# A transformer layer's hand-made instruction order: other due times for a round trip through DRAM, vector pieces between tensor pieces, another order at a seam

## The chip, the cores and the metric

The kernel runs on one core of a Trainium2 chip, with one launch. The metric is the device time of that core in microseconds (us); a profile of one execution shows what each engine did. The engines are TensorE (PE; its weight loads are shown apart as PEld), VectorE (DVE), ScalarE (ACT), GpSimd (POOL) and SyncE (SP, which here only issues DMAs). Each engine works through its own list of instructions in the order in which the program wrote them.

## The reference

Four sequences of 1024 tokens with 256 channels go through causal attention with 16 heads of 16 channels and a linear position bias, then through an encoder layer whose attention runs across the four sequences at one position, and whose feed-forward part sends each token to one of eight experts.

```python
x = L0_attn_x                                        # (4, 1024, 256)
x = x + _L0_attn_ref(_layernorm(x), w_attn, w_proj)  # causal, alibi bias, 16 heads
x = x + _L0_ffn_ref(_layernorm(x), ...)

# in _L0_ffn_ref, with T, B, C = x.shape
attn = softmax(einsum('tbhd,sbhd->bhts', q, k) * scale)
h = _layernorm(x + (ctx @ out_w.T + out_b), ln1_g, ln1_b)
_, top_i = jax.lax.top_k(softmax(flat @ router_w.T + router_b), 2)
assign = jnp.max(top_i, axis=-1)
for e in range(E):
    he = gelu(flat @ w1[e].T + b1[e]); oe = he @ w2[e].T + b2[e]
    out = where((assign == e)[:, None], oe, out)
return _layernorm(h + out, ln2_g, ln2_b)
```

(`T` is 4 there and `B` is 1024, since the encoder takes the first axis as time: its attention has four steps.)

## The kernel before

**Attention.** The queries are cut into 20 units. Units 0 to 11 are 256 queries of one sequence, units 12 to 15 the first 128 of the last 256, units 16 to 19 the other 128; four units, one for each sequence, make a position range. A unit goes through four groups of four heads. `score` multiplies keys by queries (tile `sk`) and ACT takes the exponential (`p`); `weigh` multiplies `p` by the values (`pv`) and ACT copies the result to `yt`. Along with the weighted values comes one row for each head that holds the sum of its exponentials.

**The sums' way through DRAM.** A unit's result is divided by those sums and projected. The sums lie in a few rows of `yt` and are wanted in every row, so they go through DRAM: `yt` is stored to `y`; `load_sums` loads the sums; `invert` takes the reciprocal on DVE (`inverse`) and stores it to `r`; `load_y` loads `r`, spread over the rows (`su`), and the values (`yc`); `divide` multiplies the two on DVE; `project` multiplies by the output weights on PE (`op`) and adds to `x` on DVE. All these loads and stores stand in SP's list. The last unit, 19, takes another way: `normalise(g)` spreads each group's sums with a product on PE (`sum`), takes a reciprocal and multiplies on DVE (`yn`), and `project_slots` projects. Its groups 0 and 1 do so in the loop, groups 2 and 3 after it. `load_sums(19)` is issued all the same, for a test of the sums' size at the end.

**Encoder.** Once all four units of a position range are projected, its blocks of 128 positions by four sequences can start as fronts. There are eight, 0 to 7; the last, front 7, waits for unit 19. A front is a generator that yields pieces with a kind and a cost: kind E and P for DVE, R for a root on POOL, N and A for ACT, D and d for PE. In order they are: statistics, root, normalised `u`, its transposition `ut`, q, k and v in four pieces (`qkvp`, copied to `qkv` by ACT and DVE), four scores (`pr`, `sc`), a softmax, four weightings (`pv<-qkv,sc`, `ctx`), the transposition `ct`, output projection (`ao`), a second normalisation, the routing (`key`, `before`, `equal`, `rank`, `hot`), its place among its expert's tokens (`place`). There is one `qkv` buffer: a front that wants to start its q, k, v (kind DQ) waits until the front that holds it has done its weightings. At most two fronts are under way at a time. The first six fronts admit the first table of expert tiles (`tabulate_first`, product `who_first`), and front 7 the second (`tabulate_rest`, product `who`).

**What sets the order.** The program writes the instructions in an order that an ordering model chooses while the program is built. The model has clocks for PE, DVE and ACT (`time`), advanced by the costs of the pieces. The loop goes through places: two scores, one weighing, and around them `E_slot` and `D_slot`. `attended(u, at)` puts a unit's five steps down with due times `at + SUMS_BY` and so on; `E_slot` does the DVE and DMA steps that have come due on the model's PE clock, and `D_slot` the projections that have, then calls `take_D`, which takes PE pieces of the fronts until a place holds 10 us of them (`D_SLOT`). `take_E` takes the fronts' DVE, ACT and POOL pieces that are ready, as long as the model's DVE clock is at most 1 us ahead of PE's. In the loop, `take_E` is called at the end of each `E_slot` and once after `D_slot`.

**After the loop** comes what is still due, then the rest of unit 19, and then front 7, what is left of the other fronts and of the first table, and the tiles of the experts, ordered by a second loop. A tile gathers its rows with an indirect DMA of POOL (`given`), runs `mtp`, `hid` and `oe` on PE, a normalisation on DVE with its root on POOL, and is scattered with another indirect DMA (`out_dram`).

Of the kernel before, what the change touches and what calls it, by code (L numbers as in the profile page):

```python
# [41 lines left out]
G = H // 4  # L42
# [30 lines left out]
D_SLOT = 10.0  # L73
SWITCH, COLUMN, EXP_AT_ALL, EXP, READ = 0.2, 1 / 600, 0.17, 1 / 1200, 0.7
AHEAD, EARLY_BY, ROOT, OF_D = 1.0, 0.2, 1.4, 0.35
SUMS_BY, INVERTED_BY, Y_BY, DIVIDED_BY, PROJECTED_BY = 7.0, 14.0, 18.0, 29.0, 31.0

EXP_ZERO = -126 * math.log(2.0)

# [526 lines left out]
def fast_layer(ctx: ExitStack, tc: tile.TileContext, odd, x, wq, wk, wv, wp, w_in, w_out, w_r,  # L606
# [60 lines left out]
    def bank(name):  # L667
        if tail_banks:
            return tail_banks[0].tile([P, QC], F32, tag="m", name=name)
        if half_of:  # L670
            return half_of.pop()
        pair = pair_of_banks(name)
        halves[pair.tensor.name] = [], []
        half_of.append(pair[:, 1])
        return pair[:, 0]
# [388 lines left out]
    def load_sums(u):  # L1064
        part_of_row = units[u][2] * H
        issue_stores(("y", u))
        nc.sync.dma_start(
            sums[u], heads_of(u)[:, D].rearrange("h (k w) -> h k w", w=part_of_row)
        )
# [65 lines left out]
    def normalise(g):  # L1135
        if g % 2 == 0:
            held["yn", g // 2] = ends.tile([P, 2, W], F32, tag="su", name=f"yn_{g}", bufs=2)
        yt, yn = (held[k, g // 2][:, g % 2, :P] for k in ("yt", "yn"))
        pm = bank(f"sum_{g}")[:, :P]
        nc.tensor.matmul(pm, slot_sum, yt, start=True, stop=True)  # L1140
        nc.vector.reciprocal(yn, pm)
        nc.vector.tensor_tensor(yn, yn, yt, ALU.mult)
# [894 lines left out]
    queue, running = [], []  # L2037
# [12 lines left out]
    def busy(on, cost, ready=0.0):  # L2050
        time[on] = max(time[on], ready) + cost
        return time[on]

    def on_tensor(cost):
        return busy("PE", cost, max([0.0] + [pair_free[k] for k in taken]))

    def read_at(when):
        for k in taken:
            pair_free[k] = when
        taken.clear()  # L2060

    def product(cost, what):
        taken.clear()
        what()
        end = on_tensor(cost)
        busy("DVE", OF_D * cost, end - 0.5 * cost)
        read_at(max(end + READ, time["DVE"]))
        return end

    def start_fronts():  # L2070
        if queue and len(running) < 2:
            issue_stores(*[it[0] for it in stores if it[0][0] == "u"])
        while queue and len(running) < 2:
            running.append(Running(queue.pop(0)))

    def take_E(some=True):

        start_fronts()
        left = some
        while left:  # L2080
            left = False
            for it in list(running):
                now, kind = time["PE"], it.kind
                if kind not in ("E", "N", "R", "P"):
                    continue
                on = {"E": "DVE", "P": "DVE", "N": "ACT"}.get(kind)
                if it.ready > max(now, time[on] if on else 0.0) + EARLY_BY:
                    continue
                if on == "DVE" and time["DVE"] > now + AHEAD:
                    continue  # L2090
                if kind == "R":
                    it.ready = max(now, it.ready) + ROOT
                else:
                    it.ready = busy(on, it.cost if on == "DVE" else 0.5, it.ready)
                left = True
                it.next()
                if it.kind == "end":
                    running.remove(it)

    def take_D(cost):  # L2100

        for it in list(running):
            while it.kind[0] in "Dd":
                if it.kind == "DQ" and ("qkv",) in held:
                    break
                if it.kind != "d" and it.ready > time["PE"] + EARLY_BY:
                    break
                if cost and cost + it.cost > D_SLOT:
                    break
                if it.kind == "DQ":  # L2110
                    held["qkv",] = True
                cost += it.cost
                end = product(it.cost, it.next)
                it.ready = max(end + READ, time["DVE"])
            if it.kind == "end":
                running.remove(it)

    begins = [0]
# [32 lines left out]
    due_E, due_D = [], []  # L2151
# [19 lines left out]
    def pop_due(due, now):  # L2171
        some = sorted((it for it in due if it[0] <= now), key=lambda it: it[0])
        for it in some:
            due.remove(it)
        return [(cost, what) for _, cost, what in some]
# [43 lines left out]
    def E_slot(k, some=True):  # L2219
        for cost, what in of_E.pop(k, []) + pop_due(due_E, time["PE"]):  # L2220
            what()
            busy("DVE", cost)
        issue_stores(age=1)
        for it in stores:
            it[1] += 1
        load_next()
        if tables and fetching:
            experts.fetch()
        take_E(some)

    def D_slot(p):
        todo = of_D.pop(p, []) + pop_due(due_D, time["PE"])
        for cost, what in todo:
            product(cost, what)
        take_D(sum(cost for cost, _ in todo))

    for p in range(-6, 0):
        E_slot(2 * p)
        D_slot(p)
        E_slot(2 * p + 1)  # L2240
# [9 lines left out]
    def score_next(k):  # L2250
        u, g, r = rounds[k]
        taken.clear()
        waiting.append((u, g, r, score(u, g, r)))
        end, n = on_tensor(SWITCH + columns_of(u, r) * COLUMN), columns_of(u, r)
        for pair in list(taken):
            pair_free[pair] = busy("ACT", EXP_AT_ALL + 2 * n * EXP, end)
        if r == n_rounds(u) - 1 and u < last_unit:
            to_fill.append((u + 1, g))

    def weigh_next(some):  # L2260
        taken.clear()
        weigh(some)
        end = on_tensor(SWITCH + sum(columns_of(u, r) for u, _, r, _ in some) * COLUMN)
        read_at(busy("ACT", 0.4, end))
        u, g, r, _ = some[-1]
        if g == G - 1 and r == n_rounds(u) - 1:
            attended(u, time["ACT"])

    def fill():
        while to_fill:  # L2270
            fill_slots(*to_fill.pop(0))

    for p in range(len(rounds) // 2):
        then = p < len(rounds) // 2 - 1
        score_next(2 * p)
        E_slot(2 * p)
        D_slot(p)
        fill()
        take_E(then)
        score_next(2 * p + 1)  # L2280
        if len(waiting) > 2:
            weigh_next(waiting[:2])
            del waiting[:2]
        fill()
        E_slot(2 * p + 1, then)
# [5 lines left out]


    assert not of_E and not of_D, (sorted(of_E), sorted(of_D))
    for _, what in pop_due(due_E + [], 1e9) + pop_due(due_D + [], 1e9):
        what()
    for it in running:
        it.ready = 0.0
    for g in range(2, G):
        normalise(g)
    load_sums(last_unit)  # L2300
    project_slots()
    tail = ctx.enter_context(pool("tail", 1))
# [55 lines left out]
    def begin(it):  # L2358
        if it.kind == "DQ" and ("qkv",) in held or it.kind[1:] == "C" and part.placed < NT - 1:
            return 1e9  # L2360
        return max(it.ready, free[engine_of[it.kind[0]]])
# [27 lines left out]
    while threads:  # L2389
# [4 lines left out]
        at, _, it = min((begin(it) + FIRST_BY * n, n, it) for n, it in enumerate(threads))  # L2394
# [26 lines left out]
@with_exitstack  # L2421
def tile_layer(ctx: ExitStack, tc: tile.TileContext, *args):
    nc = tc.nc
    flag = ctx.enter_context(tc.tile_pool(name="flag", bufs=1))
    odd = flag.tile([P, 1], I32, tag="odd", name="odd")
    fast_layer(tc, odd, *args)
    again = nc.values_load(
        odd[0:1, 0:1], min_val=0, max_val=1,
        skip_runtime_bounds_check_because="a comparison's result",
    )  # L2430
    with tc.If(again > 0):
        general_layer(tc, *args)
# [75 lines left out]
```

## Time and profile before

| | us |
|---|---|
| runs | 824.45, 828.9, 827.63 |
| median | 827.63 |
| the profiled execution | 827.67 |
| its span, first to last instruction | 825.9 |
| busy in the span: PE, PEld | 708.6, 532.4 |
| busy in the span: DVE, ACT, POOL | 544.8, 416.5, 253.6 |
| last `pv` product starts | 617.66 |
| unit 19 added to `x` | 632.57 |
| `who_first` | 642.87 |
| `who` | 731.59 |

A row of the profile's groups or its order of time gives start and duration, the engine, the line of the code, the operation, and what it writes and reads; in brackets stands how long the engine was idle before it and what ended the idle time. Most lines are given as L587, since a helper issues nearly all instructions; the tiles' names tell them apart. A busy PE isn't PE at its peak, and the share of busy time over the whole span mixes stages that have different limits.

### The profile page before, as it was taken

Reading aid. Unit: us, or ns where it says so; the run is one execution under the profiler, and the core shown is the slowest. Engines: PE = TensorE matmul, PEld = TensorE weight load, DVE = VectorE, ACT = ScalarE, POOL = GpSimd, SP = SyncE. Lnnn points to the kernel's source line nnn. Section 1 sums busy time; section 2 is a strip of 40 time slices with the busy share of each in tenths; the row PEclk is TensorE's granted clock in tenths of the full one; section 3 lists DMA queues with packets and bytes.
Section 4 is the critical chain, followed back from the end, with each engine's and each line's share of the span. In section 5 each row is a group of like instructions: output and inputs, shape, how many; then the busy total and the mean of one; then the engine's idle time right before and its main releaser. Section 6 shows DMA issues by size and latency. Waiting matters only on the chain. (4 is left out here: it accounts for less than half of the span.)

```text
span 825.9 us, 22497 instructions
## 1 busy us (share of the span) xinstructions
PE 708.6 (86%) x8917; PEld 532.4 (64%) x8917; DVE 544.8 (66%) x1316; ACT 416.5 (50%) x625; POOL 253.6 (31%) x360
## 2 busy tenths in 40 slices
PE   3988878999999999998998998999983689677882
PEld 2766656667666656565787876788662368566771
DVE  7335403739489768847966648497684779885663
ACT  1554535647547656635665757487550236233540
POOL 5533211313021222111222211122120235638885
PEclk9899898999999999999999999999995699988996
DMA  7444444435234234423554556255125512234430
GB/s 218 120 149 147 115 126 139 137 98 169 82 105 136 91 97 127 131 74 98 140 157 118 163 162 158 57 156 166 36 75 198 178 47 89 89 96 127 128 97 25
DMA packets 75220, 99.57 MB, mean 121 GB/s; under 512 B 19496, under 2 KB 58723, under 8 KB 74596
## 3 DMA queue, kind: packets, MB, share of 16 engines
q1 hardware_dynamic: 62272, 67.84, 28.3%
q10 hardware_dynamic: 7972, 16.05, 6.2%
q0 software_dynamic: 4864, 14.16, 5.7%
q8 instruction: 73, 1.20, 0.7%
q14 instruction: 39, 0.32, 0.1%
HBM read 61.55 MB, written 35.12 MB: 117 GB/s over the span
## 5 line engine op out<-in xcount | busy, mean ns | idle before, releaser
L587 ACT ACTIVATE p<-sk 128x1024 f32<-128x1024 f32 (+1 forms) x320 | 287.8, 939 | 160.6 <-PE sk L587 139.4
L1005 POOL TENSOR_SCALAR_AFFINE_SELECT p<-p 128x512 f32<-128x512 f32 (+1 forms) x160 | 105.6, 664 | 396.6 <-ACT p L587 394.6
L587 PE MATMUL sk<-slots 32*128 32x128 f32 (+1 forms) x3456 | 181.1, 328 | 21.5 <-DVE kq L587 8.4
L587 PEld LDWEIGHTS sk<-slots 32*128 32x128 f32 x3456 | 137.2, 187 | 65.0 <-issue 24.8
L587 PE MATMUL pv<-p,v 128*32 128x128 f32 (+1 forms) x3456 | 143.4, 312 | 9.9 <-DVE count L587 2.9
L587 PEld LDWEIGHTS pv<-p,v 128*32 128x32 f32 x3456 | 95.9, 110 | 46.9 <-issue 7.8
L587 PE MATMUL qkvp<-w_in,ut 128*128 128x264 f32 (+1 forms) x228 | 80.3, 488 | 0.0
L587 PEld LDWEIGHTS qkvp<-w_in,ut 128*128 128x128 f32 x228 | 40.8, 193 | 26.9 <-issue 22.4
L587 PE MATMUL oe<-w,ge 128*128 (+1 forms) x152 | 43.4, 410 | 14.4 <-DVE given L587 6.0
L587 PE MATMUL qkp<-xt,wqk 128*128 128x256 f32 x224 | 55.5, 392 | 0.2 <-ACT p L587 0.2
L1839 POOL DMA_INDIRECT given<-rows,rows x38 | 43.5, 1144 | 27.4 <-DVE at_t L587 11.4
L587 DVE COPY qkv<-qkvp 128x264 f32<-128x264 f32 x28 | 12.1, 432 | 54.1 <-PE qkvp L587 54.1
L587 PEld LDWEIGHTS qkp<-xt,wqk 128*128 128x128 f32 x224 | 40.9, 191 | 10.5 <-issue 3.3
L587 PE MATMUL hid<-mt,w 128*128 128x128 f32 x304 | 47.2, 293 | 0.4 <-ACT ge L587 0.4
L587 ACT COPY qkv<-qkvp 128x512 f32<-128x512 f32 (+1 forms) x29 | 16.1, 557 | 59.0 <-PE qkvp L587 47.1
L587 PEld LDWEIGHTS hid<-mt,w 128*128 128x128 f32 x304 | 42.2, 201 | 1.9 <-ACT ge L587 0.9
L1955 POOL DMA_INDIRECT out_dram<-o,out_rows x38 | 38.9, 1024 | 8.7 <-issue 5.9
L587 DVE TENSOR_TENSOR pv<-qkv,sc 128x1024 f32<-128x1024 f32 x32 | 40.2, 1257 | 0.6 <-PE ctp L587 0.6
L587 DVE TENSOR_REDUCE sc<-pr 128x64 f32<-128x1024 f32 x32 | 39.0, 1220 | 1.1
L587 DVE TENSOR_TENSOR pr<-qkv 128x1024 f32<-128x1024 f32 x32 | 39.6, 1238 | 0.0
L587 PEld LDWEIGHTS oe<-w,ge 128*128 128x128 f32 x152 | 27.2, 200 | 19.1 <-DVE given L587 7.4
L587 PE MATMUL vp<-wv,xt 128*128 128x256 f32 x128 | 34.4, 414 | 0.0
(316 smaller groups left out, 1017.9 us busy)
## 6 DMA issues: line engine op xcount, KB each, us to landing
slots<-k SPq DMA_DIRECT2D x128, 80.0 KB
k<-kq SPq DMA_DIRECT2D x32, 256.0 KB
v<-v ACTq DMA_DIRECT2D x4, 1152.0 KB
x<-in_x_dram SPq DMA_DIRECT2D x16, 256.0 KB
y<-yt SPq DMA_DIRECT2D x16, 256.0 KB
rows<-x SPq DMA_DIRECT2D x32, 128.0 KB
slots<-k SPq DMA_DIRECT2D x64, 64.0 KB
rows<-u SPq DMA_DIRECT2D x8, 512.0 KB
```

The costliest lines, as they stand in the source:

```text
L587: ins = made(*args, **kwargs)
L1005: nc.gpsimd.affine_select(blocks, blocks, pattern=[[0, 2], [0, size], [1, P]], compare_op=ALU.is_ge, fill=0.0, base=0, channel_multiplier=-1,)
L1839: nc.gpsimd.indirect_dma_start(out=self.hx, out_offset=None, in_=t.rows_of, in_offset=bass.IndirectOffsetOnAxis(ap=t.rows_[:, self.j:self. ...
L1955: ins = nc.gpsimd.indirect_dma_start(out=out.rearrange("t n c -> (t n) c"), out_offset=bass.IndirectOffsetOnAxis(ap=t.table.out_rows[:, t. ...
```

## The change

It has three parts. The five due times of a unit's way become shorter. `take_D` calls `take_E` after each PE piece that it takes, where before only the end of the place did; `some` says whether vector pieces may be taken (not in the last place of the loop). And after the loop, `normalise(2)` and `normalise(3)` are written ahead of the projections that are still due, but behind the loads and divisions that are still due; before, they stood behind both.

```diff
-SUMS_BY, INVERTED_BY, Y_BY, DIVIDED_BY, PROJECTED_BY = 7.0, 14.0, 18.0, 29.0, 31.0
+SUMS_BY, INVERTED_BY, Y_BY, DIVIDED_BY, PROJECTED_BY = 5.0, 10.0, 12.5, 19.0, 20.5

-    def take_D(cost):
+    def take_D(cost, some):
         for it in list(running):
             while it.kind[0] in "Dd":
...
                 cost += it.cost
                 end = product(it.cost, it.next)
+
                 it.ready = max(end + READ, time["DVE"])
-            if it.kind == "end":
+                take_E(some)
+            if it.kind == "end" and it in running:
                 running.remove(it)

-    def D_slot(p):
+    def D_slot(p, some=True):
         todo = of_D.pop(p, []) + pop_due(due_D, time["PE"])
         for cost, what in todo:
             product(cost, what)
-        take_D(sum(cost for cost, _ in todo))
+        take_D(sum(cost for cost, _ in todo), some)

         E_slot(2 * p)
-        D_slot(p)
+        D_slot(p, then)
         fill()

-    for _, what in pop_due(due_E + [], 1e9) + pop_due(due_D + [], 1e9):
+    for _, what in pop_due(due_E + [], 1e9):
+        what()
+    for g in range(2, G):
+        normalise(g)
+    for _, what in pop_due(due_D + [], 1e9):
         what()
     for it in running:
         it.ready = 0.0
-    for g in range(2, G):
-        normalise(g)
     load_sums(last_unit)
     project_slots()
```

## The prediction

> **What bounds the kernel now.** I read first the page's slices and a table of windows, which share the run out by stage, then the waits of VectorE (DVE) inside attention, then the order of time around the seam between attention and the last stage. The kernel has three regimes: attention to about 620 us, a seam of 12 us, and a last stage of some 200 us. The columns of the table are: stretch, its length, then busy us of PE, PEld, DVE, ACT, POOL with instruction counts, the granted clock, the DMA share and GB/s.
>
> ```profile
> 500.00:620.00 120.00, 111.76 (x2384) 89.65 (x2384) 88.42 (x187) 75.70 (x99) 24.80 (x39) 0.99 0.37 105
> 620.00:632.00 12.00, 6.20 (x24) 4.75 (x16) 3.19 (x6) 0.27 (x1) 0.00 (x0) 0.50 0.62 214
> 632.00:666.00 34.00, 19.31 (x80) 10.82 (x79) 24.82 (x66) 6.49 (x12) 5.49 (x5) 0.74 0.45 153
> 666.00:732.00 66.00, 54.61 (x364) 47.17 (x364) 59.11 (x159) 29.42 (x63) 32.34 (x33) 0.92 0.28 84
> 732.00:800.00 68.00, 53.59 (x381) 46.58 (x378) 43.88 (x138) 27.59 (x61) 54.73 (x75) 0.95 0.39 118
> ```
>
> Attention belongs to PE (111.8 of 120 us), and DVE has 31.6 us to spare there. From 632 to 732 us it is DVE: 83.9 of 100 us, and in its second part 59.1 of 66. From 732 us it is POOL (54.7 of 68), which gathers rows for the expert tiles and scatters results. The chain that ended last says the same: it can be followed back only to DVE's work at 716 us, goes through the `who` product of the second table at 731.6 us, and from there along POOL. So the end is set by when `who` can run, and `who` needs the routing of the last encoder block, front 7.
>
> Next, DVE's waits between 200 and 620 us (who waited, for whom: us in all, times, longest):
>
> ```profile
> DVE qkv L587 <- PE qkvp L587: 45.4, 21, 6.1
> DVE yc L587 <- DMA yc<-y: 12.5, 4, 5.8
> DVE inverse L587 <- DMA sums<-y: 4.9, 2, 3.8
> ```
>
> DVE's idle time in attention is mostly that inside a run of encoder products: PE projects q, k, v token group by token group and DVE has nothing queued between the copies. Meanwhile encoder vector work is queued behind that run, and what is left of it at 620 us is done in the DVE-bound stage. The order of time shows both ends:
>
> ```profile
> 587.01 0.43 DVE L587 COPY qkv<-qkvp 128x264 f32<-128x264 f32 x1 [0.37 <-PE qkvp L587]
> 589.73 0.43 DVE L587 COPY qkv<-qkvp 128x264 f32<-128x264 f32 x1 [2.29 <-PE qkvp L587]
> 592.45 0.43 DVE L587 COPY qkv<-qkvp 128x264 f32<-128x264 f32 x1 [2.29 <-PE qkvp L587]
> 592.80 0.18 DVE L587 TENSOR_REDUCE best<-key 128x4 f32<-128x32 f32 x1
> ...
> 617.66 2.74 PE L587 MATMUL pv<-p,v 128*32 128x128 f32 x64 [2.86 <-DVE count L587]
> 620.45 0.27 ACT L587 COPY yt<-pv 128x128 f32<-128x128 f32 x1 [5.24 <-PE pv L587]
> ...
> 625.67 0.43 DVE L587 TENSOR_TENSOR yc<-yc,su 128x256 f32<-128x256 f32 x1 [6.71 <-DMA yc<-y]
> 628.71 0.96 DVE L587 RECIPROCAL yn<-sum 128x128 f32<-128x128 f32 x1
> 632.57 0.42 DVE L587 TENSOR_TENSOR x<-x,op 128x256 f32<-128x256 f32 x1 [1.38 <-PE op L587]
> ...
> 642.44 1.22 DVE L587 TENSOR_TENSOR pv<-qkv,sc 128x1024 f32<-128x1024 f32 x1
> 655.51 1.07 ACT L587 COPY qkv<-qkvp 128x512 f32<-128x512 f32 x2 [11.81 <-DVE pv L587]
> ```
>
> Two gaps of 2.29 us stand between copies, then a burst of vector work. After 620 us DVE waits 6.7 us for unit 18's `yc`. Front 6's weighting (`pv<-qkv,sc`, four times from 642.44) comes after the end of attention, and ACT waits 11.8 us to copy front 7's q, k, v, because the one `qkv` buffer is still read by front 6.
>
> **What the Trainium skill says.** "PSUM — Partial Sum Buffer", Engine vs sequencer instructions: the queues of ScalarE, VectorE and GpSimdE are strict FIFO. The trace agrees: vector work ready before 587 us stands behind the copies and starts at 592.80. "DMA: Bandwidth & Descriptors", Anatomy of one DMA: a semaphore wait happens on the issuing sequencer before dispatch, and a DMA on GpSimd's path has about 2.0 us fixed. Here, on SP's queue, unit 18's `r` store was issued at 618.99 and the first load that needs it at 621.19 us: 2.2 us. "Perfetto Trace Analysis", Optimization Strategy: with several regimes, interleaving them may help; the table above shows the regimes.
>
> **The change part by part.** (1) The due times set only the order of instructions. From a unit's last weighing, sums, inverse, loads, division and projection now come at 5, 10, 12.5, 19, 20.5 instead of 7, 14, 18, 29, 31 of the model's us. A place of the schedule costs the model 4 us (single-block units: two scores of 0.2+512/600 and a weighing of 0.2+1024/600) to some 13 us (with encoder products), so 10.5 us are one or two places. Fronts 4, 5 and 6, which start from the projections of units 11 and 15, can start that much earlier. What the way itself needs, from the trace: store issue 0.4, landing 2.2, issue 0.55, landing 2.2, reciprocal 0.24 to 0.35, issue 0.35, landing 2.2, four loads 2.5, landing 2 (yc issued by 623.7, divided at 625.67), about 13 us. The order fits on average. Where two steps fall into one visit, DVE waits; the bounds are nothing and 3.8 us for an inverse, 5.8 us for a division (the longest waits above).
>
> (2) Vector pieces are now taken between products. No instruction is added. A gap of 2.29 us is about one score or weighting piece (1.22+1.22 us, or 1.22+0.69+0.42). Over 200 to 620 us 45.4 us of gaps can be filled. The cost: a PSUM copy queues behind up to one such piece, 2.4 us, while PE has other bank pairs to write; without that cover PE waits 2 us for each of the 28 qkv copies on DVE, 56 us at the very worst; I take nothing.
>
> What follows from (1) and (2): each front holds the one `qkv` buffer for less time, and 4, 5 and 6 follow one another through it. By the model's own order of the kernel before, front 6 takes `qkv` about four places before the end of attention, and fronts 4 and 5 hold it seven places each. One to two places from the start of front 4, and about one saved per hold, put front 6 three to four places further on: through its softmax and weighting, up to its `ct`. Front 5, whose end admits the first table, ends about three places earlier, so that table falls into attention too.
>
> Moved out of the last stage, from DVE's rows of 633 to 658 us: top and subtract 1.0, softmax sums 1.5, four weightings of 1.22+0.69+0.42 = 9.3, copy of `ct` 0.7, first table 1.3+2.0+1.5+2.6 = 7.4: 19.9 us. DVE is 84% busy there, so I pass on three quarters, 15 us. The 11.8 us wait for `qkv` is part of this, not added to it. Against it, front 7 finishing earlier leaves about one more tile for POOL after `who`: an out 1.0, a gather 1.1, a memset 0.1, half a root 0.4, gaps 0.3: 2.9 us. Last stage: -12 us (bounds -20, -3).
>
> PE work moved into attention: eight transposes of `ct`, 1.9 us, and `who_first`, 1.3 us. Against this stand the 2.9 us that PE waited for DVE at 617.66, if that backlog goes. Attention: +2 us (bounds -4, +8).
>
> (3) The seam. Today 620.72 (end of the last `yt` copy) to the `x` addition at 632.57 is 11.9 us: wait for `yc`, project unit 18 (2.05), then the sums of groups 2 and 3, two reciprocals with products (628.71 to 631.19), last products. Now the sums come first, 1.1 us of PE, and the 2.5 us of DVE run beside unit 18's projection; with `yc` there the `x` addition follows at 620.7+1.1+2.5+1.4 = 625.7, 6.9 us sooner. If `yc` is as late as today, PE still stands before unit 18's products until 626.2, and only 1 us is won. The loads are due at 12.5 rather than 18, so they go out a visit or two before the end: I take -5 us (bounds -7, -1). SP's loads of expert weights behind `load_sums` aren't needed before 668 us.
>
> Sum: +2 - 12 - 5 = -15 us against the profiled execution's 827.67 us (span 825.9 plus 1.8 around), which stands at the median of 827.63: 812.7, so 813 us. Its own range is 803 to 823.
>
> **The rivals.** *Given back after `who`*: earlier routing finds more tiles of the first table undone; five more at 2.9 us eat 14.5 of the 15 us, which leaves +2 - 5 = -3: about 825 us. For it: POOL is 80% busy after 732 us. Against: the first table comes earlier too, and POOL stands idle for most of 620 to 670 us.
> *The order hardly moves*: front 6 stands where it stood, since `qkv` and not the projection holds it. 827 us. For it: front 5 waits for the buffer for several places. Against: part (2) shortens just those holds.
> *Slower, DVE waits for landings in attention*: if inverse and division fall into one visit with their loads for most of the 19 units, DVE loses 3.8+5.8 = 9.6 us a unit, 182 us instead of the 50 us of today (30.7 for sums, 19.2 for `yc`). The PSUM copies stand behind it; at one fifth reaching PE, 132 us more make +26 us. Then the forecast's -15 is overrun: 827.67+26-15, about 839 us. It decides once these waits pass about 125 us in all (75 more at a fifth make 15). For it: steps of 5 and 6.5 us are shorter than a place with encoder products. Against: in 200 to 620 us PE waited only about 11 us for DVE (its own table of waits), so most such stalls were absorbed. That the code doesn't do what it says I leave at almost nothing.
>
> **How the numbers follow.** Forecast 0.50, given back 0.16, order unmoved 0.14, slower 0.20. The range 801 to 833 takes in the first three and the near end of the fourth. What a measurement here can tell from no change is 0.5%, 4.1 us: below 823.5 lie nearly all of the forecast and a part of the second, 0.62; between 823.5 and 831.8 the rest of these and the third, 0.18; above, the fourth, 0.20.
>
> **What would show it.** Right: waits `qkv<-qkvp` of DVE clearly under 45 us; `who` about 15 us or more before 731.6; front 6's weighting and `who_first` before the last `pv`; no 11.8 us wait of ACT; sums before unit 18's `op`. Wrong: `sums` and `yc` waits of DVE over 125 us, PE's busy share of 200 to 620 us falling under 93%, the last `pv` later than 628 us, or as long a way as today from the last `pv` to `who`.

## The result, and the profile after

The changed kernel takes 855.52 us (median of 4 runs, 850.01 to 863.67) against 827.15 us for the kernel before beside it: a ratio of 1.0324, with a 95% interval of 1.0257 to 1.039. One of the four runs, 863.67 us, was in a slower state of the chip; the ratios here, and the medians from here on, leave such runs out. The change costs some 27 us, where a gain of 14 us, 813 us, was foretold.

The table of windows by stage, first of the kernel before and then of the changed one. Columns: stretch, length, busy us of PE, PEld, DVE, ACT and POOL with instruction counts, granted clock, DMA share, GB/s. The cuts are the end of the last `yt` copy (the end of attention) and the start of the product `who`.

```profile
0.00:620.70 620.70, 565.06 (x8019) 414.32 (x8019) 402.19 (x914) 350.06 (x482) 146.59 (x223) 0.98 0.43 125
620.70:731.50 110.80, 79.22 (x440) 62.27 (x440) 86.62 (x230) 35.44 (x76) 37.83 (x38) 0.82 0.37 120
731.50:826.00 94.50, 64.29 (x459) 55.83 (x458) 56.03 (x173) 31.01 (x69) 69.13 (x99) 0.90 0.30 94
```

```profile
0.00:663.90 663.90, 581.07 (x8043) 426.94 (x8043) 412.39 (x948) 349.75 (x483) 147.33 (x224) 0.95 0.40 117
663.90:761.40 97.50, 75.43 (x417) 60.57 (x418) 75.56 (x196) 35.20 (x75) 35.49 (x38) 0.89 0.41 136
761.40:855.70 94.30, 64.82 (x458) 55.85 (x458) 56.57 (x173) 30.56 (x69) 69.22 (x99) 0.90 0.31 94
```

Attention is 43.2 us longer (663.9 against 620.7), the stretch from there to `who` 13.3 us shorter (97.5 against 110.8), and what follows `who` the same. 43.2 - 13.3 - 0.1 = 29.8, which is the difference of the two spans (855.7 - 825.9). The profiled execution took 857.52 us, some 4 us more than the median of those kept. So the loss is all in attention, and a gain is where one was expected. Inside attention PE's idle time rose from 620.7 - 565.1 = 55.6 to 663.9 - 581.1 = 82.8 us, 27.2 more; the other 16.0 us are busy time, for only 24 matmuls more (the first table, 0.81 us together). The granted clock tells why: its mean fell from 0.98 to 0.95. In the trace's records of that clock it is at half for 68.3 us of attention against 25.9 before, and PE is busy in those stretches for 51.4 us against 18.8; a projection product takes 634 ns there and 379 otherwise (last section), so an estimate of the loss is 40 to 50% of the difference, 13 to 16 us. The split into idle and busy is exact only to some 7 us: seam_only, below, has the same order in attention as the kernel before, and shows 571.9 us busy at 0.96 (before 565.1 at 0.98), with attention ending at 620.1.

Next the waits, from 20 us to the end of attention, of DVE and then of PE (who waited, for whom: us, times, longest). First the kernel before:

```profile
DVE qkv L587 <- PE qkvp L587: 54.1, 25, 6.1
DVE inverse L587 <- DMA sums<-y: 30.7, 6, 14.6
...
DVE yc L587 <- DMA yc<-y: 12.5, 4, 5.8
```

```profile
PE xtp L587 <- DVE xn L587: 4.2, 3, 3.2
PE qkp L587 <- DVE xn L587: 3.6, 1, 3.6
```

Then the changed one:

```profile
DVE yc L587 <- DMA yc<-y: 57.2, 10, 9.9
DVE qkv L587 <- PE qkvp L587: 41.8, 21, 2.3
...
DVE inverse L587 <- DMA sums<-y: 20.9, 6, 5.7
...
DVE yc L587 <- DMA sums<-y: 7.7, 1, 7.7
```

```profile
PE xtp L587 <- DVE xn L587: 16.7, 5, 8.8
PE qkp L587 <- DVE yc L587: 8.5, 3, 5.7
PE vp L587 <- DVE yc L587: 6.3, 1, 6.3
...
PE router L587 <- DVE yc L587: 2.4, 1, 2.4
PE op L587 <- DVE yc L587: 2.2, 1, 2.2
```

A wait for several signals is put down to the one that came last, so a wait of the division (`yc`) can stand under another load's name, as `sums` here. DVE's waits for landings (`yc` and `inverse`) went from 43.2 to 85.8 us. PE waited 7.8 us for `xn` and 1.7 for `yc` before; now 16.7 and 19.4. (`qkp`, `vp`, `router` and `xtp` name the PSUM bank: the product that reads `yc` is the projection, whichever bank it gets.) Its waits for other work of DVE fell from 23.7 to 13.8 us, so that DVE held up PE for 49.9 us in all, 33.2 before.

One place shows the whole thing. The order of time of the changed kernel, cut to one unit's way and to what waited ("..." stands for lines left out):

```profile
298.60 0.34 DVE L587 RECIPROCAL inverse<-sums 128x32 f32<-128x32 f32 x1
...
298.97 0.34 SPq L1075 DMA_DIRECT2D r<-inverse  x1
300.44 0.60 SPq L1090 DMA_DIRECT2D su<-r  x1
...
302.35 0.57 SPq L1093 DMA_DIRECT2D yc<-y  x1
...
306.79 0.69 DVE L587 TENSOR_TENSOR yc<-yc,su 128x512 f32<-128x512 f32 x1 [7.85 <-DMA yc<-y]
307.40 1.38 DVE L587 TENSOR_SCALAR u<-u,mv_h,rstd_h 128x256 f32<-128x256 f32 x4
...
309.80 0.73 DVE L587 TENSOR_SCALAR xn<-x,mv_x,rstd_x 128x256 f32<-128x256 f32 x2
...
310.36 1.13 PE L587 MATMUL xtp<-ident,xn 128*128 128x128 f32 x4 [8.82 <-DVE xn L587]
```

The reciprocal, its store, the four loads and the division stand back to back in the program. The last load was issued at 302.35 us and DVE's next instruction after the reciprocal is the division, which starts at 306.79: 7.85 us in which DVE does nothing. Behind it stand four `u`, five small instructions and then `xn`, the normalised rows that PE is to transpose next. PE's next product needs `xn`, and PE stands 8.82 us. The windows around it, with the columns of above:

```profile
295.00:301.50 6.50, 6.45 (x111) 4.12 (x100) 3.70 (x15) 5.40 (x7) 2.99 (x4) 1.00 0.17 43
301.50:310.00 8.50, 0.04 (x2) 0.00 (x0) 3.10 (x11) 1.51 (x2) 1.28 (x2) 0.63 0.30 96
310.00:315.00 5.00, 4.64 (x24) 3.71 (x28) 4.27 (x15) 0.58 (x1) 0.00 (x0) 0.61 0.37 108
315.00:320.00 5.00, 5.00 (x67) 3.23 (x60) 3.91 (x7) 3.70 (x5) 0.00 (x0) 1.00 0.29 103
```

PE is busy 0.04 of 8.5 us, and then works at a mean clock of 0.61 for five more: part of the stall is paid a second time in slow products.

The seam, in order of time:

```profile
663.65 0.27 ACT L587 COPY yt<-pv 128x128 f32<-128x128 f32 x1 [1.91 <-PE pv L587]
663.80 0.57 SPq L1093 DMA_DIRECT2D yc<-y  x1
...
668.00 0.43 DVE L587 TENSOR_TENSOR yc<-yc,su 128x256 f32<-128x256 f32 x1 [5.47 <-DMA yc<-y]
...
673.07 0.42 DVE L587 TENSOR_TENSOR x<-x,op 128x256 f32<-128x256 f32 x1 [1.72 <-PE op L587]
```

Unit 18's last load goes out at 663.80, after the last copy of attention, and DVE waits 5.47 us for it (6.71 before): from 663.9 to the `x` addition 9.2 us, 11.9 before. Front 6's weighting (`pv<-qkv,sc`) still comes after that, at 673.40, 678.85 and 681.29; one of its four came before.

### The profile page after: what moved, and what is told of

Its sections match the earlier page's. It is cut to its first block, busy times and chain, and to the rows that moved or that the text cites. A ratio compares the mean times of both kernels' runs of the same rounds, so it can differ in the third digit from the quotient of the medians.

```text
span 855.7 us, 22492 instructions
## 1 busy us (share of the span) xinstructions
PE 721.3 (84%) x8917; PEld 543.4 (63%) x8917; DVE 544.5 (64%) x1316; ACT 415.5 (49%) x625; POOL 252.1 (29%) x360
## 5 line engine op out<-in xcount | busy, mean ns | idle before, releaser
L1005 POOL TENSOR_SCALAR_AFFINE_SELECT p<-p 128x512 f32<-128x512 f32 (+1 forms) x160 | 102.6, 645 | 443.1 <-ACT p L587 441.4
L587 PE MATMUL sk<-slots 32*128 32x128 f32 (+1 forms) x3456 | 183.0, 331 | 18.8 <-DMA slots<-kq 3.5
L587 PEld LDWEIGHTS sk<-slots 32*128 32x128 f32 x3456 | 139.8, 192 | 62.4 <-issue 25.4
L587 PE MATMUL qkvp<-w_in,ut 128*128 128x264 f32 (+1 forms) x216 | 72.7, 472 | 0.0
L587 PE MATMUL qkp<-xt,wqk 128*128 128x256 f32 x224 | 57.8, 404 | 0.2 <-ACT p L587 0.2
L587 DVE TENSOR_TENSOR yc<-yc,su 128x512 f32<-128x512 f32 (+1 forms) x19 | 11.8, 622 | 70.3 <-DMA yc<-y 62.6
L587 PEld LDWEIGHTS qkvp<-w_in,ut 128*128 128x128 f32 x216 | 38.4, 190 | 25.7 <-issue 21.2
L587 PE MATMUL oe<-w,ge 128*128 (+1 forms) x152 | 42.9, 406 | 11.8 <-DVE mv_v L587 5.3
L1839 POOL DMA_INDIRECT given<-rows,rows x38 | 41.5, 1091 | 23.9 <-DVE at_t L587 14.0
L587 DVE COPY qkv<-qkvp 128x264 f32<-128x264 f32 x28 | 11.9, 429 | 41.8 <-PE qkvp L587 41.8
```

Of the source, the lines that this page charges most:

```text
L587: ins = made(*args, **kwargs)
L1005: nc.gpsimd.affine_select(blocks, blocks, pattern=[[0, 2], [0, size], [1, P]], compare_op=ALU.is_ge, fill=0.0, base=0, channel_multiplier=-1,)
L1839: nc.gpsimd.indirect_dma_start(out=self.hx, out_offset=None, in_=t.rows_of, in_offset=bass.IndirectOffsetOnAxis(ap=t.rows_[:, self.j:self. ...
```

## The experiments

Four theories were set against each other. **A**: short due times put a division, and sometimes a reciprocal, on VectorE before its loads have landed, and VectorE's list stands. **B**: vector pieces between products delay the PSUM copies, and PE waits for banks. **C**: only the two together do harm. **D**: the projection comes due before `yc` is divided, and TensorE's own list stands at it. A, B and C were set up before the first runs, D after them.

All kernels are the one before or the changed one with the edits shown; due times are given in the order sums, inverse, loads, division, projection. "Attention" is the end of the last `yt` copy, "x" the start of the last `x` addition, `who` its start, all in the profiled execution.

| kernel | median us | ratio to before, 95% | attention | x | `who` | span |
|---|---|---|---|---|---|---|
| before | 827.15 | | 620.7 | 632.6 | 731.5 | 825.9 |
| changed | 853.52 | 1.0324 [1.0257, 1.039] | 663.9 | 673.1 | 761.4 | 855.7 |
| times_only | 863.95 | 1.0407 [1.0346, 1.0468] | 661.1 | 668.5 | 768.8 | 862.9 |
| pieces_only | 833.27 | 1.0079 [1.0059, 1.01] | 621.8 | 632.9 | 731.6 | 826.2 |
| seam_only | 826.98 | 0.9992 [0.9974, 1.001] | 620.1 | 630.3 | 731.3 | 826.0 |
| late_divide | 816.28 | 0.987 [0.9836, 0.9905] | 615.8 | 619.6 | 719.4 | 814.2 |
| div19_proj31 | 836.25 | 1.0109 [1.0046, 1.0171] | 634.4 | 641.9 | 740.3 | 834.5 |
| div24_proj25 | 828.58 | 1.0016 [0.9994, 1.0037] | 633.6 | 637.5 | 733.1 | 827.8 |
| pool_divide | 859.26 | 1.0369 [1.0298, 1.044] | 663.3 | 672.1 | 761.4 | 858.1 |
| late_divide_no_pieces | 814.27 | 0.9845 [0.9805, 0.9886] | 614.8 | 618.7 | 717.3 | 811.7 |
| pool_div19_proj31 | 821.13 | 0.9927 [0.99, 0.9954] | 611.9 | 619.9 | 721.6 | 818.4 |
| late_no_pieces_old_seam | 816.94 | 0.988 [0.9849, 0.9911] | 615.7 | 620.6 | 720.8 | 815.2 |
| div30_no_pieces | 816.54 | 0.9857 [0.9814, 0.9899] | 615.9 | 619.9 | 721.2 | 815.9 |
| pool_late_no_pieces | 825.44 | 0.9981 [0.9961, 1.0001] | 619.5 | 623.4 | 723.8 | 820.8 |

### Each part alone

times_only is the kernel before with the new due times and nothing else:

```diff
-SUMS_BY, INVERTED_BY, Y_BY, DIVIDED_BY, PROJECTED_BY = 7.0, 14.0, 18.0, 29.0, 31.0
+SUMS_BY, INVERTED_BY, Y_BY, DIVIDED_BY, PROJECTED_BY = 5.0, 10.0, 12.5, 19.0, 20.5
```

> The kernel before with the five short due times alone. Theory A (the short times put reciprocals and divisions on VectorE ahead of the landing of their loads; VectorE's list stands, TensorE runs dry behind it): 840 to 858 us, VectorE's waits for sums and yc together 85 us or more, last pv 20 to 40 us later than in the kernel before. Theory B (vector pieces between the encoder's products delay the copies that TensorE needs): 820 to 828 us, as the seam and the earlier fronts may gain a little. Theory C (only both together are slow): 822 to 832 us.

863.95 us: the times alone cost 4.1%, no less than the whole change. Attention ends at 661.1, 40.4 us late. That excludes B and C as the cause of the loss. It doesn't fit A well either: the time is above A's range, and DVE's waits for landings, 67.3 us, are below the 85 that A wanted. PE waits 25.4 us for `yc`, 1.7 before: the first sign of D.

pieces_only is the changed kernel with the old times and the old seam, so only the middle part of the diff is in it, whose working line is:

```diff
                 it.ready = max(end + READ, time["DVE"])
+                take_E(some)
```

> The kernel before with vector pieces taken between the encoder's products alone, old due times, old seam. Theory A: 812 to 826 us, VectorE's waits for sums and yc at 50 us or less, its waits for qkvp under 45 us. Theory B: 840 to 858 us, with TensorE waiting for copies of VectorE. Theory C: 820 to 830 us.

833.27 us, 0.8% slower, and outside the ranges of all three theories. Its profiled execution was the shortest of its 11 runs (827.94 to 835.56) and shows stage ends within 1.1 us of before, so the trace doesn't show where the 0.8% lies. What it does show is that the gaps stayed: DVE's waits for `qkvp` from 20 us to the end of attention are 48.5 us, against 54.1 before.

seam_only is the kernel before with the new order after the loop:

```diff
-    for _, what in pop_due(due_E + [], 1e9) + pop_due(due_D + [], 1e9):
+    for _, what in pop_due(due_E + [], 1e9):
+        what()
+    for g in range(2, G):
+        normalise(g)
+    for _, what in pop_due(due_D + [], 1e9):
         what()
     for it in running:
         it.ready = 0.0
-    for g in range(2, G):
-        normalise(g)
```

> The kernel before with the last unit's sums written ahead of unit 18's projection alone. All three theories: 1 to 3 us less than before, 824 to 827 us, since unit 18's yc lands as late as it did and TensorE stands in front of its products; no change before the last pv.

827.0 us, ratio 0.9992 with an interval that holds 1: no change to be measured. The way from attention to `x` shrinks from 11.9 to 10.2 us in the profile, and DVE there still waits 7.27 us for unit 18's `yc`. The new order brings little while the loads are late.

### The last two times put back

late_divide is the changed kernel with the early loads kept and the division and projection at their old times:

```diff
-SUMS_BY, INVERTED_BY, Y_BY, DIVIDED_BY, PROJECTED_BY = 5.0, 10.0, 12.5, 19.0, 20.5
+SUMS_BY, INVERTED_BY, Y_BY, DIVIDED_BY, PROJECTED_BY = 5.0, 10.0, 12.5, 29.0, 31.0
```

> The changed kernel with the division and projection due at 29 and 31 again, sums, inverse and loads still at 5, 10 and 12.5. Theory A, with the division as the step that costs: 820 to 832 us, waits for yc under 20 us, waits for sums still 20 to 30 us. Theory B: 850 to 860 us, nothing regained. Theory C: 835 to 850 us.

816.28 us: from 3.2% slower to 1.3% faster than before, and faster than A's range. Its waits of DVE, same view and stretch as above:

```profile
DVE inverse L587 <- DMA sums<-y: 38.4, 8, 11.4
...
DVE yc L587 <- DMA yc<-y: 1.3, 1, 1.3
```

The `yc` waits are gone (64.9 us to 1.3). The waits for `sums` are not: they are larger than in the changed kernel and than A expected, and attention is still 4.9 us shorter than before. So the loss sits in the last two due times, not in the first three. Which of the two, this run can't tell.

### Division or projection

div19_proj31 and then div24_proj25 are the changed kernel with other last times:

```diff
-SUMS_BY, INVERTED_BY, Y_BY, DIVIDED_BY, PROJECTED_BY = 5.0, 10.0, 12.5, 19.0, 20.5
+SUMS_BY, INVERTED_BY, Y_BY, DIVIDED_BY, PROJECTED_BY = 5.0, 10.0, 12.5, 19.0, 31.0
```

> The changed kernel with the division still due at 19 and the projection due at 31. Theory A (a division on VectorE ahead of its loads holds up VectorE's list): 835 to 850 us, waits of VectorE for yc 40 us or more, TensorE's waits for xn as in the changed kernel, those for yc near zero. Theory D (what costs is the projection, which TensorE's list meets before yc is divided): 812 to 822 us, as with both late, although VectorE waits as much for yc.

836.25 us, in A's range and above D's. DVE waits for landings about as long as in the changed kernel, but attention ends 29.5 us earlier. The waits of DVE and then of PE for `xn` or `yc`:

```profile
DVE yc L587 <- DMA yc<-y: 44.1, 9, 12.3
...
DVE inverse L587 <- DMA sums<-y: 20.3, 5, 4.9
...
DVE yc L587 <- DMA sums<-y: 8.1, 1, 8.1
DVE yc L587 <- DMA slots<-k: 6.4, 1, 6.4
DVE yc L587 <- DMA v<-v: 4.5, 1, 4.5
```

```profile
PE xtp L587 <- DVE xn L587: 7.5, 5, 5.2
```

DVE's waits come to 83.4 us, 85.8 in the changed kernel; PE's wait for `yc` is gone. So, taken apart in this order, 29.5 us of the changed kernel's attention hang on the projection's due time, and 634.4 - 615.8 = 18.6 us on that of the division (against late_divide, where DVE's waits for landings are 39.7 us). These 18.6 us, too, show at PE: it waits 29.8 us for DVE in all, for `u`, `xn`, `kq` and `ut` above all, and 15.0 in late_divide.

```diff
-SUMS_BY, INVERTED_BY, Y_BY, DIVIDED_BY, PROJECTED_BY = 5.0, 10.0, 12.5, 19.0, 20.5
+SUMS_BY, INVERTED_BY, Y_BY, DIVIDED_BY, PROJECTED_BY = 5.0, 10.0, 12.5, 24.0, 25.5
```

> The changed kernel with division and projection due at 24 and 25.5, half way. Theory A: the time follows how many divisions still meet loads that have not landed: 818 to 835 us, waits for yc between 5 and 30 us. Theory D: 825 to 845 us, since the projection comes nearly as close to the loads as in the changed kernel.

828.58 us, the same as before and in the ranges of both theories, so it doesn't decide between them. `yc` waits of DVE are down to 15.8 us (10.3 and 5.5), but attention is still 12.9 us longer than before; the way to `x` (8.0 us shorter) and the one from there to `who` (3.3) make up for it. One wait of PE for `yc` takes 9.8 us; PE's idle time in attention is 4.8 us above before, and its busy time 8.1 (573.2 against 565.1), at a clock of 0.96. That a single stop of PE brings all of this isn't shown.

### The division moved to GpSimd

pool_divide is the changed kernel with the multiplication on another engine, so that VectorE's list has no division to stand at:

```diff
-        nc.vector.tensor_tensor(yc, yc, su, ALU.mult)
+        nc.gpsimd.tensor_tensor(yc, yc, su, ALU.mult)
```

> The changed kernel with the division on GpSimd instead of VectorE, all due times as in the changed kernel. Theory A: the wait stands in another list, so VectorE's yc waits vanish and TensorE's waits for xn with them: 815 to 835 us, unless GpSimd's masks queue behind the division. Theory D: 845 to 860 us, since TensorE meets the projection as early as before.

859.26 us: no better than the changed kernel, where A expected 815 to 835. Theory A alone has fallen; D alone fell with div19_proj31. POOL now stands at the loads, and PE at POOL; the order of time of one unit, and PE's waits in attention:

```profile
411.94 1.26 POOL L1098 TENSOR_TENSOR yc<-yc,su 128x512 f32<-128x512 f32 x1 [6.15 <-DMA yc<-y]
...
413.25 3.66 PE L587 MATMUL xtp<-wp,yc 128*128 128x256 f32 x8 [5.19 <-POOL yc L1098]
```

```profile
PE op L587 <- POOL yc L1098: 12.9, 9, 3.1
PE xtp L587 <- POOL yc L1098: 11.7, 2, 6.5
PE qkp L587 <- POOL yc L1098: 10.5, 3, 6.4
PE vp L587 <- POOL yc L1098: 9.5, 1, 9.5
PE router L587 <- POOL yc L1098: 3.3, 1, 3.3
```

Those are 47.9 us. With VectorE rid of the division, PE meets the projection directly, and stands.

pool_div19_proj31 adds the late projection to it:

```diff
-SUMS_BY, INVERTED_BY, Y_BY, DIVIDED_BY, PROJECTED_BY = 5.0, 10.0, 12.5, 19.0, 20.5
+SUMS_BY, INVERTED_BY, Y_BY, DIVIDED_BY, PROJECTED_BY = 5.0, 10.0, 12.5, 19.0, 31.0
```

> The changed kernel with the division on GpSimd at 19 and the projection at 31. If both walls count, VectorE's list before an early division and TensorE's list before an early projection: with both out of the way 812 to 824 us, about as with both late, and no wait of VectorE for yc. If a division at 19 costs for another reason than the place where it waits (the order it brings to the rest): 830 to 840 us, as with the early division on VectorE.

821.13 us. The division stands at its loads as in pool_divide (POOL's waits, below), and in attention PE doesn't wait for it at all:

```profile
POOL yc L1098 <- DMA yc<-y: 55.7, 10, 11.2
POOL yc L1098 <- DMA v<-v: 6.5, 1, 6.5
POOL yc L1098 <- DMA y<-yt: 2.8, 1, 2.8
```

Attention ends 51.4 us earlier than in pool_divide (611.9 against 663.3), and PE's 47.9 us of waits are gone: nearly all of what the early projection costs there is PE standing at it.

These runs make a square. Medians in us, all with the early loads, the vector pieces and the new seam:

| | projection at 20.5 | projection at 31 |
|---|---|---|
| division at 19 on VectorE | 853.52 | 836.25 |
| division at 19 on GpSimd | 859.26 | 821.13 |
| division at 29 on VectorE | | 816.28 |

Both walls count, and one hides the other. With an early projection, it makes no difference that can be told here whether VectorE stands (853.5 and 859.3, with overlapping intervals of their ratios). With a late one, VectorE's stand costs 15.1 us (836.3 - 821.1). An early projection costs 17.3 us on top of an early division on VectorE, and 38.1 us without it. So the loss has no fixed split: A alone can't explain it, since without D its remedy brings nothing, and D alone can't, since 15 us stay. In attention the projection is the larger part (29.5 of 48.1 us, or 51.4 with the division on GpSimd). In the whole time the two steps on VectorE are about equal, 17.3 and then 20.0 us (836.3 - 816.3), since with the late projection the gain of the last stage goes, as told below.

pool_late_no_pieces shows what moving the multiplication costs by itself: it is late_divide_no_pieces, below, with the line of pool_divide.

> The best version so far (due times 5, 10, 12.5, 29, 31, new order at the seam, no vector pieces between tensor pieces; 814.27 us), with the division on GpSimd instead of VectorE. If the division costs nothing but its 0.4 to 0.7 us on VectorE once its operands have landed (theories A and D: late steps find landed data), 810 to 817 us, with no wait of TensorE for yc above 2 us in attention. If VectorE's list was still held up by the divisions in the best version, under 810 us. If the slower multiplication on GpSimd pushes yc behind the projection, 820 us or more, with waits of TensorE for POOL's yc.

825.44 us against 814.27. The multiplication takes 1267 ns at the median on POOL and 682 on DVE (19 of them, of two sizes), PE waits 5.7 us for POOL's `yc` in attention, and attention ends 4.7 us later. In the profiles the kernel is 9.1 us longer: besides these 4.7 us, 1.8 between `x` and `who` and 2.6 after `who`, where there is no division; the cause of those stays open. So the GpSimd row of the square probably carries some cost of its own, though with the early division that wasn't measured.

### Without the pieces, without the seam

late_divide_no_pieces is the kernel before with the new seam (the diff of seam_only) and the first of these lines; late_no_pieces_old_seam has that line alone; div30_no_pieces has the new seam and the second line.

```diff
-SUMS_BY, INVERTED_BY, Y_BY, DIVIDED_BY, PROJECTED_BY = 7.0, 14.0, 18.0, 29.0, 31.0
+SUMS_BY, INVERTED_BY, Y_BY, DIVIDED_BY, PROJECTED_BY = 5.0, 10.0, 12.5, 29.0, 31.0
```

```diff
-SUMS_BY, INVERTED_BY, Y_BY, DIVIDED_BY, PROJECTED_BY = 7.0, 14.0, 18.0, 29.0, 31.0
+SUMS_BY, INVERTED_BY, Y_BY, DIVIDED_BY, PROJECTED_BY = 5.0, 10.0, 12.5, 30.5, 32.0
```

> The kernel before with sums, inverse and loads at 5, 10 and 12.5, division and projection at 29 and 31, and the new order at the seam, but no vector pieces between products. If the pieces are worth what the run without the other parts showed (0.8 per cent slower): 808 to 816 us. If they pay once the division is late: 820 to 830 us.

> The kernel before with sums, inverse and loads at 5, 10 and 12.5 alone; division, projection, pieces and seam as before. If the seam's order pays once unit 18's loads are early: 816 to 820 us, 2 to 5 us more than with the new seam, and 6 to 8 us from the last yt copy to the last addition to x. If the early loads alone bring the gain at the seam: 813 to 816 us.

> As the version with late division and no pieces, but division and projection due at 30.5 and 32. If more room after the loads still pays: 808 to 812 us. If at 29 no division meets its loads any more: 813 to 819 us, the fronts starting a little later.

814.27, 816.94 and 816.54 us. The first is the best of all kernels here, and beats both that this case began with: 0.9845 of the time of before. Its seam in order of time:

```profile
612.26 0.43 DVE L587 TENSOR_TENSOR yc<-yc,su 128x256 f32<-128x256 f32 x1
614.56 0.27 ACT L587 COPY yt<-pv 128x128 f32<-128x128 f32 x1 [6.91 <-PE pv L587]
617.80 0.41 DVE L587 TENSOR_TENSOR x<-x,op 128x256 f32<-128x256 f32 x1
618.68 0.42 DVE L587 TENSOR_TENSOR x<-x,op 128x256 f32<-128x256 f32 x1 [0.46 <-PE op L587]
```

Unit 18 is divided at 612.26, before the last copy of attention: the way to `x` is 3.9 us (11.9 before). With the old seam it is 4.9. So of the 8.0 us the early loads bring 7 and the new order 1 in the profiles; the medians (816.94 and 814.27, with overlapping intervals of their ratios) can't tell such a difference. Attention itself is 5.9 us shorter. From `x` to `who` 98.6 us, as before (98.9). Pieces between products add nothing that can be seen to this version (late_divide, 816.28). Still later steps bring nothing more (div30_no_pieces).

## Why the prediction was wrong

**The failed step: attention at +2 us, bounds -4 to +8, with no term for the stops that the shorter times bring.** It measured +43.2. Three things in its working were wrong.

First, the projection was costed at nothing. The step named the DVE waits that a division and a reciprocal could bring, and asked what is queued behind them on DVE. It moved the projection as well, from 31 to 20.5 of the model's us, and never asked what is queued behind that: on PE, everything. With its due time back at 31, attention is 29.5 us shorter (div19_proj31), the larger part of the 43.2; and it is 38 us of the median once VectorE is out of the way (pool_divide against pool_div19_proj31). The way itself was reckoned a little short. From the reciprocal to the division the terms come to some 7.4 us (0.3, 0.35, 2.2, 2.5, 2); it took 8.2 us at 298.60 to 306.79, with 4.4 us from the last load's issue to its use, and 9.7 us for unit 18 (658.31 to 668.00). The whole way of 13 us was not measured. The last two steps followed the loads by a model clock that knows no landing.

Second, the share of DVE's waits that reaches PE. The prediction took waits as absorbed, and in its slower rival a fifth of them as reaching PE, without a working; beside it stood the 11 us that PE waited for DVE before. Between late_divide and div19_proj31 DVE's waits rise by 43.7 us and attention by 18.6: 0.43. From before to changed, with the projection moved too, 42.6 us more waits came with 43.2 us more attention.

Third, the sum had no term for the clock. Of the 43.2 us some 27 are idle PE and some 16 slower products, to within the 7 us named above.

**The slower rival had the direction, not the mechanism.** It wanted 9.6 us of waits a unit, 182 us, and put the deciding point at 125 us in all. The waits were 85.8 us in attention, and the kernel was slower all the same. Its point failed because it rested on the fifth; and it looked for the harm at the PSUM copies, where PE's main waits were for `xn` and `yc`.

**Vector pieces in the gaps.** Expected: fronts three to four places further on, 19.9 us of DVE work moved out, waits for `qkvp` clearly under 45 us from 200 us on. This sign came: 33.2 us from there to the end of attention, 45.4 before. But front 6's weighting was not moved: three of four come after the end of attention. The piece that follows a product is ready only `READ`, 0.7 us, after it, and `take_E` right behind the product admits what is ready within `EARLY_BY`, 0.2 us; unless the model's DVE clock is 0.5 us ahead of PE's, the piece isn't eligible there. That this is why gaps stayed is read from the code, not shown by a run. The first table did move: its product runs at 657.4 us, before the last `pv` (642.9 before, after it). DVE's work between the end of attention and `who` fell by 11.1 us (86.6 to 75.6), not 19.9.

**The last stage: -12, measured -10.6** (`x` to `who` 98.9 to 88.3), ACT's 11.8 us wait for `qkv` gone, `who` to the end unchanged. The size was right, but what it hangs on was not foreseen: neither the pieces with late division (99.8) nor the times alone (100.3) have it, and with the pieces and the early division but a late projection it is gone too (98.4, div19_proj31). pool_divide has it (89.3). So it takes both the pieces and the early projection, since fronts 4 to 6 begin from projected units, and was bought with the very projections that cost 29.5 us. In late_divide the rival "the order hardly moves" describes this stage.

**The seam: -5 with bounds -7 and -1, measured -2.7,** and -1.7 with the new order alone, as the case of a late `yc` in the prediction says. The -5 needed loads that land before attention ends: late_divide, with the same due times for them but a late division and projection, won 8.1 (3.8 us from 615.8 to 619.6).

**Of the signs that were named:** `who` came at 761.4 and not before 716, the last `pv` ended at 663 us, later than the 628 named, PE's busy share from 200 to 620 us was 89% (375.5 of 420), under the 93% named: two of the signs of being wrong came. The waits over 125 us didn't, and the way from the last `pv` to `who` was shorter than before.

813 us was in the end about the time of the best version (814.27). That is chance: its terms are others, attention -5.9, seam -8.0, last stage nothing.

## What to carry to other kernels

In a list that an engine works through in order, the due time of a step that consumes a transfer is a bet on when it lands, and losing it stops everything written behind the consumer; issue such loads early and place the consumers late, and treat the two as separate knobs. When a step is moved forward, ask of each of its instructions, on each engine, what stands behind it: the consumer of the consumer can be the greater cost. And a stop of TensorE can cost more than its own length; look at the granted clock after it.

The Trainium skill says the first half in "DMA: Bandwidth & Descriptors", Rules for kernel authors: issue the DMA early, compute, and wait on its semaphore late. These runs agree, with 816.28 us for late waits and 853.52 for early ones on the same loads.

## What the runs showed of the hardware

The price of a short stop of TensorE was not expected. In the changed kernel the gap of 8.8 us at 301.5 is followed by five microseconds at a mean clock of 0.61. The group rows of the projection's products, all of one shape, show it too (operation, out<-in and count, then ns least, median, most, and first and last start):

```profile
L587 PE MATMUL op<-wp,yc x68: 379/379/634, 86.9 to 669.6; 128*128 128x256 f32 x68
...
L587 PE MATMUL xtp<-wp,yc x16: 379/634/635, 311.3 to 413.0; 128*128 128x256 f32 x16
```

379 ns is the usual time of a projection product; those in bank `xtp` are two units' projections that come just behind stops of 8.8 and 6.3 us, and take 634 at the median. In attention the trace's records have the granted clock either full or at half, and at half for whole multiples of 3.41 us. At these two stops and one of 5.7 us at 454.0, half rate begins 2.1, 3.1 and 3.3 us after PE's last product and ends 3.6, 3.7 and 4.4 us after the next one starts. The Trainium skill's "TensorE: Matmul & The Clock Gate", Part 1: The HAM clock gate (the "warmup" mystery), states half rate after an idle window of about 3.4 us and full rate after about 3.4 us of sustained work. The trace agrees roughly in both, but half rate came up to 1.3 us sooner than that. Nor does the length of a stop alone decide: one of 2.15 us at 601.7, where PE waited for `yc`, was followed by 3.4 us at half rate, and one of 2.79 us at 585.1 by none. Over attention it came to some 16 us for 27 us of added gaps.

Also new: on GpSimd, busy for 166 of the 612 us of attention, standing at landings showed no cost there (65 us of POOL's waits in pool_div19_proj31, with attention ending 8.8 us before that of the kernel before), though the multiplication itself is nearly twice as long on it.
